# AUGRU keys of a recommendation model: transposed two steps ahead in six buffers, and gathered a step earlier

## The chip, the cores and the metric

The kernel runs on one NeuronCore of a Trainium2 chip. The metric is the time of one execution on the device in microseconds; a smaller number is better. The engines are named as in the profile: PE is TensorE (its weight loads are a row of their own, PEld), DVE is VectorE, ACT is ScalarE, POOL is GpSimd, SP is SyncE. All arithmetic is in 32-bit floats.

## The reference

1024 samples each have a history of 100 items with 128 features. Three stages follow one another: a GRU over the history, attention over its outputs, and a second recurrent network (AUGRU) over the same outputs, whose update gate is scaled by the attention. The state that AUGRU has at the end of each sample's sequence goes into a small network that gives the score.

```python
# gru: h_t for all t, from zero
keys = gru_seq                                   # [1024, 100, 128]
feat = concat([keys, q, keys - q, q * keys])     # q: item_embedding
score = mlp(feat, [512 -> 80, 80 -> 40, 40 -> 1], relu)
attn = softmax(where(mask == 1, score, -inf), over t)
pooled = einsum('bt,btd->bd', attn, keys)
att_seq = pooled.T[:100]

def augru_step(h, x_t, a_t):                     # x_t = keys[:, t], a_t = att_seq[t]
    r = sigmoid(concat([h, x_t]) @ Wr.T + br)
    u = sigmoid(concat([h, x_t]) @ Wu.T + bu)
    h_hat = tanh(concat([h * r, x_t]) @ Wh.T + bh)
    u = a_t[:, None] * u
    return (1 - u) * h + u * h_hat

attention_feature = aug_out[b, sequential_length[b] - 1]
comb = concat([user, item, hist_sum, item * hist_sum, attention_feature])
return mlp(comb, [640 -> 200, 200 -> 80, 80 -> 1], sigmoid)
```

The weight `a_t` of an AUGRU step is a feature of the pooled vector, so AUGRU can't start before all keys are pooled.

## The kernel before

The 128 features lie on the partitions, the samples along the free dimension. The 1024 samples are two halves (`NH = 2`) of `HB = 512` columns, which are worked on in turn so that the engines have one half to work on while the other waits. `gru_phase` runs the first recurrence and the attention over both halves and stores the keys in DRAM, by groups of steps: `READ` is the number of steps in each group (4, 4, then eleven times 8, then 4) and `FIRST` the first step of each (0, 4, 8, 16, ... 88, 96). `augru_phase`, which the change touches, runs the second recurrence. It begins at about 1440 us of the profiled 2085.5.

For AUGRU the samples are sorted by length, longest first, so that a late step computes only the columns of samples that are still alive. `widths[t]` is the number of columns that step `t` computes in each half: it falls from 512 to 96. (A value computed on the device picks one of three such plans; with these inputs it is the first, the narrowest.)

How a key reaches PE. The sort makes it necessary to gather the rows of the keys from DRAM, each row holding one sample's keys, or a 32-feature part of them, for all steps of a group. `load_rows` (L144) does this with indirect DMAs that POOL issues (L159), each after a small copy on POOL from the tile `rest` of the step then running (L158), which paces them. `gathers(q)` is the sequence of all such DMAs of group `q`, and `spread(q)` says how many of them are issued after each half step, so that the group is complete some steps before its first use. The rows are then transposed, one step and half at a time, by `load_key` (L996 to L1013) into a tile `k3` of 128 x 512 from the pool `qp3`. For the first two groups (`q < WHOLE`, steps 0 to 7) PE transposes blocks of 128 x 128 into the single PSUM buffer of the pool `pa3` (L1006) and ACT copies the result (L1007). For all later steps DVE does it alone, in blocks of 32 x 32 (L1010).

The step itself is `half_step(t, i)` for half `i`. The engines run in program order: the program is written out by hand, no scheduler reorders it. Each half step does the following.

- PE closes `ph` of the other half, the half step before (`ph<-r`, L1024), then `pr` and `pu` of its own half (`pr<-h`, `pu<-h`, L1024); ACT takes the tanh `c` of the first and the sigmoids of the others.
- DVE multiplies `u` and `c` of the other half (L1048), makes `r` (L1050), updates the other half's state `h3` (L1052), scales `pu` with the attention (L1058) and makes `rest` (L1061).
- PE opens the three gates of the half step after (`open_gates`, `pr<-k`, `ph<-k`, `pu<-k`, L1020): the part of the matmul that depends only on the key.
- The attention weights of two steps later are loaded (`load_att`), and the key of one step later in the same half is transposed (`load_key(t + 1, i)`).

So PE has six matmuls in each half step, each with its own weights; the profile shows each as a pair (`x2`).

Ahead of the loop stand, in this order: the keys of step 0, ACT's four stores of the last `pooled` rows, the gathers of the attention weights in sorted order (`att_r`, L135), the first step (L947), the keys of step 1, the gates of step 1, its first weights, and the gathers of group 1. Scores of samples that have ended are computed beside the loop in small portions (`predict`, L1080 to L1148); they gather and scatter through POOL too (L1088).

The tile pools of the AUGRU phase take over the memory that the pools of the GRU phase used; where an AUGRU tile lies over a GRU tile, its first writer waits until that tile's last reader is done.

Of the kernel before, what the change touches and what calls it, by code (L numbers as in the profile page):

```python
# [21 lines left out]
T = 100  # L22
HB = 512
NH = B // HB
# [31 lines left out]
FIRST = [sum(READ[:q]) for q in range(len(READ))]  # L56
# [16 lines left out]
def kernel(ctx: ExitStack, tc: tile.TileContext, a: dict, out: bass.AP):  # L73
# [70 lines left out]
    def load_rows(q, i, width, tiles):  # L144

        n = READ[q]
        if q < WHOLE:
            tag = "whole" if q else "once"
            r = rows[q, i] = tiles.tile([P, GH, n * P], F32, tag=tag, name="rows", bufs=NH)
            for g in range(GH):  # L150
                gather(r[:, g, :], keys_d[q], g, i)
                yield
            return
        r = rows[q, i] = tiles.tile([P, KH, n * R], F32, tag="rows", name="rows")
        for k in range(-(-width // R)):
            if later.get("pace") is not None:

                nc.gpsimd.tensor_copy(r[:, k, 0:1], later["pace"])  # L158
            nc.gpsimd.indirect_dma_start(  # L159
                out=r[:, k, :],  # L160
                out_offset=None,
                in_=keys_d[q],
                in_offset=bass.IndirectOffsetOnAxis(ap=idx_k[:, k, i : i + 1], axis=0),
            )
            yield

    def all_of(steps):
        for _ in steps:
            pass
# [755 lines left out]
    def augru_phase(pools, widths, alive):  # L925


        wp = pools.enter_context(tc.tile_pool(name="wp3", bufs=3))
        qp = pools.enter_context(tc.tile_pool(name="qp3", bufs=4))
        sp = pools.enter_context(tc.tile_pool(name="sp3", bufs=2))  # L930
        kp = pools.enter_context(tc.tile_pool(name="kp3", bufs=4))
        ps = pools.enter_context(tc.tile_pool(name="ps3", bufs=7, space=PSUM))
# [37 lines left out]
        def first_state(i, p):  # L970
            weight_row(0, i, p)
            u, h = gates[i]
            nc.vector.tensor_mul(p, p, u)
            nc.vector.tensor_mul(h3[i], p, h)

        def first_weights(i, p):
            weight_row(1, i, p)
            at = att[1, i] = wp.tile([P, HB], F32, name="at", bufs=6)
            nc.scalar.copy(at, p)

        def store_weights(i, p):

            for g in range(GH):
                nc.tensor.transpose(p[:, ts(g, P)], sorted_rows[i][:, g, :], ident)
            rows_t = wp.tile([P, HB], F32, name="att_t", bufs=2)
            nc.vector.tensor_copy(rows_t, p)
            nc.sync.dma_start(out=att_d[i], in_=rows_t[:T, :])
            load_att(2, i)

        def load_att(t, i):  # L990
            w = widths[t]
            at = wp.tile([P, HB], F32, name="at", bufs=6)
            nc.sync.dma_start(
                out=at[:, :w], in_=att_d[i][t, :w].partition_broadcast(P)
            )
            att[t, i] = at  # L996

        def load_key(t, i):

            q = max(j for j, first in enumerate(FIRST) if first <= t)  # L1000
            w, n, r = widths[t], t - FIRST[q], rows[q, i]
            k = qp.tile([P, HB], F32, name="k3")
            if q < WHOLE:
                p = pa.tile([P, HB], F32, tag="a", name="pk3")
                for g in range(-(-w // P)):
                    nc.tensor.transpose(p[:, ts(g, P)], r[:, g, ts(n, P)], ident)  # L1006
                nc.scalar.copy(k[:, :w], p[:, :w])  # L1007
            else:
                w = -(-w // R)
                nc.vector.transpose(  # L1010
                    k.rearrange("p (k r) -> p k r", r=R)[:, :w, :], r[:, :w, ts(n, R)]
                )
            keys[t, i] = k  # L1013

        def open_gates(t, i):

            k = keys.pop((t, i))[:, : widths[t]]
            for m, name in ((wr, "pr"), (wh, "ph"), (wu, "pu")):
                p = opened[t, i, name] = bank(name)[:, : widths[t]]
                nc.tensor.matmul(p, lhsT=m[:, 1, :], rhs=k, start=True, stop=False)  # L1020

        def close_gate(t, i, name, m, v):
            p = opened.pop((t, i, name))
            nc.tensor.matmul(p, lhsT=m[:, 0, :], rhs=v, start=False, stop=True)  # L1024
            return p

        def open_state(t, i):

            r, u, rest = resets.pop((t, i))
            ph = close_gate(t, i, "ph", wh, r)  # L1030
            c = wp.tile([P, HB], F32, name="c3")[:, : widths[t]]
            nc.scalar.activation(c, ph, AF.Tanh, bias=later["bh"])  # L1032
            states[i] = u, c, rest, h3[i][:, : widths[t]]

        def half_step(t, i):


            w, h = widths[t], h3[i][:, : widths[t]]
            before, after = ((t - 1, 1), (t, 1)) if i == 0 else ((t, 0), (t + 1, 0))
            if before in resets:  # L1040
                open_state(*before)
            pr = close_gate(t, i, "pr", wr, h)
            pu = close_gate(t, i, "pu", wu, h)
            nc.scalar.activation(pr, pr, AF.Sigmoid, bias=later["br"])
            nc.scalar.activation(pu, pu, AF.Sigmoid, bias=later["bu"])
            state = states.pop(1 - i, None)
            if state is not None:
                nc.vector.tensor_mul(state[0], state[0], state[1])  # L1048
            r = wp.tile([P, HB], F32, name="r3")[:, :w]
            nc.vector.tensor_mul(r, h, pr)  # L1050
            if state is not None:
                nc.vector.tensor_sub(state[3], state[0], state[2])  # L1052
            if t == 1 and i == 0:
                store_weights(0, pa.tile([P, HB], F32, tag="a", name="pw"))
                first_state(1, spare)
            elif t == 1:
                first_weights(1, spare)
            nc.vector.tensor_mul(pu, pu, att.pop((t, i))[:, :w])  # L1058
            rest = wp.tile([P, HB], F32, name="rest")[:, :w]

            nc.vector.scalar_tensor_tensor(  # L1061
                out=rest, in0=pu, scalar=1.0, in1=h, op0=ALU.subtract, op1=ALU.mult
            )
            later["pace"] = rest[:, 0:1]
            resets[t, i] = r, pu, rest
            if after[0] < T and (*after, "pr") not in opened:
                open_gates(*after)
            if t == 1 and i:
                store_weights(1, spare)
            if t + 2 < T:  # L1070
                load_att(t + 2, i)
            if t + 1 < T:
                load_key(t + 1, i)

        def last_state(i):
            u, c, rest, h = states.pop(i)
# [73 lines left out]
        def gathers(q):  # L1150
            for i in range(NH):
                yield from load_rows(q, i, widths[FIRST[q]], kp)

        def spread(q):


            ahead = 2 if widths[FIRST[q]] > HB // 2 else 3
            n = NH * -(-widths[FIRST[q]] // R)
            slots = NH * (FIRST[q] - (FIRST[q - 1] if q > 2 else 1) - ahead)
            done = [-(-j * n // slots) for j in range(slots + 1)]  # L1160
            return [b - a for a, b in zip(done, done[1:])]

# [12 lines left out]
        first_state(0, pa.tile([P, HB], F32, tag="a", name="first"))  # L1175
        first_weights(0, spare)
        all_of(gathers(1))
        ahead, due = gathers(2), spread(2)
        jobs, final = [], None
        for t in range(1, T):  # L1180
            if t in FIRST[2:-1]:
                all_of(ahead)
                ahead, due = gathers(FIRST.index(t) + 1), spread(FIRST.index(t) + 1)
            for i in range(NH):
                half_step(t, i)
                for _ in range(due.pop(0) if due else 0):
                    next(ahead, None)

                for n, job in enumerate(list(jobs)):
                    job[0] += 1  # L1190
                    if n == 0 and job[0] > 2 * G and next(job[1], job) is job:
                        jobs.remove(job)
            left = alive[t + 1] if t + 1 < T else 0
            for g in range(1, HB // PR):
                if left <= g * PR < alive[t]:
                    jobs.append([0, predict(g)])
                    if left:
                        next(jobs[-1][1])
            if t == T - G:
                final = predict(0, last=True)  # L1200
                next(final)
# [10 lines left out]
    def augru(n):  # L1212
        with ExitStack() as pools, tc.manual_schedule():
            augru_phase(pools, WIDTHS[n], ALIVE[n])
# [75 lines left out]
```

## Time and profile before

| | |
|---|---|
| time, median of 3 runs | 2083.58 us (2083.48 to 2083.83) |
| span of the profiled execution | 2085.5 us |
| instructions | 26811 |
| mean granted clock of TensorE | 0.993 |
| DMA traffic | 205.09 MB, mean 98 GB/s |
| read from and written to HBM | 147.16 MB, 54.40 MB |

The five engines' busy shares stand in the profile line with which the prediction begins. A busy share is an average over stages: in the GRU phase and in the first two thirds of the AUGRU phase PE has no room at all, in the last third of the AUGRU phase, where the steps are narrow, it has a little. A row of a timeline gives the start in microseconds, the duration, the engine, the line of the kernel, the operation, the tile written and those read, the shapes, and in brackets the idle time of the engine before it and what ended that.

### The profile page before, as it was taken

The page shows a single profiled execution, that of the slowest core. Times are in us where ns is not written, and L with a number is a line of the kernel's source. Part 1 is how long each engine was busy: PE and PEld are TensorE (multiplying, and loading weights), DVE is VectorE, ACT ScalarE, POOL GpSimd, SP SyncE. Part 2 cuts the span into 40 slices and gives each one's busy share as a digit, 9 for nine tenths or more (in the row PEclk, how much of TensorE's full clock was granted, in tenths as well). Part 3 has the DMA queues.
Part 4 walks back from the last instruction along what each step waited for, and adds up shares of the span by engine and source line. Part 5 has one row for each costly group of instructions (what it writes and reads, how often), then busy time and mean ns, then how long its engine had stood idle before and what let it go on. Part 6 is the DMA issues. An engine that isn't in the chain of part 4 may idle for free. (4 is left out here: it accounts for less than half of the span.)

```text
span 2085.5 us, 26811 instructions
## 1 busy us (share of the span) xinstructions
PE 2039.8 (98%) x8320; PEld 980.6 (47%) x8320; DVE 1755.5 (84%) x3050; ACT 831.7 (40%) x1516; POOL 1304.6 (63%) x1306
## 2 busy tenths in 40 slices
PE   8999999999999999999999999997899999999997
PEld 3343333333333333333333333333444556678897
DVE  6888999989989888989889899997467777888786
ACT  3334343333434333433333343333343444445454
POOL 0234939579796959595969687986635444444332
PEclk9999999999999999999999999998999999999999
DMA  4633233332234334333433222332533333334331
GB/s 119 114 93 100 90 102 110 95 98 84 89 106 112 109 103 121 110 95 110 132 98 102 82 81 89 102 93 72 150 95 110 97 93 96 98 98 97 78 73 35
DMA packets 254324, 205.09 MB, mean 98 GB/s; under 512 B 75814, under 2 KB 216842, under 8 KB 254170
## 3 DMA queue, kind: packets, MB, share of 16 engines
q1 hardware_dynamic: 239738, 170.57, 29.2%
q0 software_dynamic: 12320, 32.44, 5.6%
q8 instruction: 68, 1.11, 0.2%
q14 instruction: 86, 0.70, 0.1%
q10 hardware_dynamic: 2112, 0.26, 0.1%
HBM read 147.16 MB, written 54.40 MB: 97 GB/s over the span
## 5 line engine op out<-in xcount | busy, mean ns | idle before, releaser
L490 PE MATMUL ps<-x,wih 128*128 128x512 f32 x1200 | 592.6, 603 | 4.0 <-DMA x<-in_hist_x 4.0
L490 PE MATMUL ps<-hn,whh 128*128 128x512 f32 x1188 | 574.4, 592 | 0.0
L490 PEld LDWEIGHTS ps<-x,wih 128*128 128x128 f32 x1200 | 220.9, 191 | 327.5 <-issue 253.0
L490 PEld LDWEIGHTS ps<-hn,whh 128*128 128x128 f32 x1188 | 225.7, 190 | 284.1 <-issue 275.8
L476 POOL TENSOR_TENSOR xm<-x,m 128x512 f32<-128x512 f32 x200 | 247.2, 1236 | 136.3 <-DMA m<-mask_d 136.0
L521 ACT ACTIVATE ps<-ps,bih 128x512 f32<-128x512 f32 x200 | 132.4, 662 | 486.6 <-DVE ps L520 486.6
L502 ACT ACTIVATE r<-ps,brz 128x512 f32<-128x512 f32 x200 | 137.5, 687 | 372.9 <-PE ps L490 372.1
L477 POOL TENSOR_TENSOR hist<-hist,xm 128x512 f32<-128x512 f32 x200 | 266.7, 1333 | 15.7
L587 POOL TENSOR_TENSOR pooled<-pooled,kw 128x512 f32<-128x512 f32 x191 | 254.4, 1332 | 15.0
L586 POOL TENSOR_TENSOR kw<-kt,e 128x512 f32<-128x512 f32 x191 | 219.3, 1148 | 70.3 <-DVE e L759 70.2
L159 POOL DMA_INDIRECT rows<-keys_d,idx_k x208 | 202.3, 973 | 83.8 <-POOL rows L158 53.0
L563 DVE TENSOR_TENSOR kq<-hn,item 128x512 f32<-128x512 f32 x200 | 228.5, 1182 | 0.0
L650 PE MATMUL pm<-hn,wk 128*32 128x512 f32 x1200 | 212.0, 596 | 3.5 <-ACT q L233 1.8
L650 PE MATMUL pm<-kq,wkq 128*32 128x512 f32 x1200 | 209.6, 592 | 0.0
L1032 ACT ACTIVATE c<-ph,bh 128x96 f32<-128x96 f32 (+42 forms) x198 | 96.9, 489 | 262.2 <-PE ph L1024 227.7
L650 PE MATMUL pm<-mv,w 128*32 128x512 f32 (+1 forms) x808 | 196.5, 598 | 1.4 <-DVE e L740 1.4
L158 POOL COPY rows<-rest 128x1 f32<-128x1 f32 x208 | 39.1, 188 | 222.1 <-DVE rest L1061 218.1
L1048 DVE TENSOR_TENSOR pu<-pu,c 128x96 f32<-128x96 f32 (+42 forms) x197 | 88.8, 451 | 103.6 <-ACT c L1032 85.0
L684 DVE TENSOR_TENSOR f<-pm,q 128x512 f32<-128x512 f32 x200 | 128.3, 683 | 51.2 <-PE pm L650 51.1
L525 DVE TENSOR_TENSOR d<-hn,ps 128x512 f32<-128x512 f32 x198 | 135.9, 687 | 34.8 <-ACT ps L521 32.5
L526 DVE TENSOR_TENSOR d<-ps,d 128x512 f32<-128x512 f32 x200 | 138.4, 692 | 23.6 <-ACT ps L522 6.4
L520 DVE TENSOR_TENSOR ps<-ps,u 128x512 f32<-128x512 f32 x200 | 140.0, 700 | 21.6 <-PE ps L490 0.5
(180 smaller groups left out, 3028.3 us busy)
## 6 DMA issues: line engine op xcount, KB each, us to landing
x<-in_hist_x SPq DMA_DIRECT2D x212, 256.0 KB
keys_d<-kt SPq DMA_DIRECT2D x46, 1024.0 KB
m<-mask_d SPq DMA_DIRECT2D x200, 128.0 KB
keys_d<-kt SPq DMA_DIRECT2D x64, 64.0 KB
rows<-keys_d,idx_k POOLq DMA_INDIRECT x208
s_b<-mv SPq DMA_DIRECT2D x200, 8.0 KB
mask_i<-in_mask SPq DMA_DIRECT2D x8, 200.0 KB
at<-att_d SPq DMA_DIRECT2D x32, 48.0 KB
```

The source lines that it names most:

```text
L159: nc.gpsimd.indirect_dma_start(out=r[:, k, :], out_offset=None, in_=keys_d[q], in_offset=bass.IndirectOffsetOnAxis(ap=idx_k[:, k, i : i + ...
L476: nc.gpsimd.tensor_mul(d, x, m)
L477: nc.gpsimd.tensor_add(acc, acc, d)
L490: nc.tensor.matmul(p, lhsT=w[:, g, :], rhs=v, start=(j == 0), stop=(j == len(parts) - 1),)
L502: nc.scalar.activation(r, pr, AF.Sigmoid, bias=brz[:, 0:1])
L520: nc.vector.tensor_add(pi, pi, u)
L525: nc.vector.tensor_sub(d, h, pi)
L526: nc.vector.tensor_mul(d, pz, d)
L563: nc.vector.tensor_mul(kq, h, item[:, self.cols])
L586: eng.tensor_mul(d, k, w)
L587: eng.tensor_add(acc, acc, d)
L650: nc.tensor.matmul(p[i][s, :], lhsT=w[:, s], rhs=v, start=start, stop=stop)
```

## The change

The key of a half step is transposed two steps ahead, where it was one, and the pool of the key tiles grows from four buffers to six, since two more tiles are alive at any time. The keys of step 2 are therefore transposed ahead of the loop. Since a group's rows are needed one step earlier, the loop turns to the next group one step earlier too (`t + 1` in place of `t`), and `spread` counts with that. It is for the wait of PE for a key: with the change a gate's key has been ready a whole step when PE opens the gate.

```diff
-        qp = pools.enter_context(tc.tile_pool(name="qp3", bufs=4))
+        qp = pools.enter_context(tc.tile_pool(name="qp3", bufs=3 * NH))
...
-            if t + 1 < T:
-                load_key(t + 1, i)
+            if t + 2 < T:
+                load_key(t + 2, i)
...
         def spread(q):
-            ahead = 2 if widths[FIRST[q]] > HB // 2 else 3
+            ahead = 3 if widths[FIRST[q]] > HB // 2 else 4
             n = NH * -(-widths[FIRST[q]] // R)
-            slots = NH * (FIRST[q] - (FIRST[q - 1] if q > 2 else 1) - ahead)
+            slots = NH * (FIRST[q] - (FIRST[q - 1] - 1 if q > 2 else 1) - ahead)
...
         all_of(gathers(1))
+        for i in range(NH):
+            load_key(2, i)
         ahead, due = gathers(2), spread(2)
         jobs, final = [], None
         for t in range(1, T):
-            if t in FIRST[2:-1]:
+            if t + 1 in FIRST[2:-1]:
                 all_of(ahead)
-                ahead, due = gathers(FIRST.index(t) + 1), spread(FIRST.index(t) + 1)
+                ahead, due = gathers(FIRST.index(t + 1) + 1), spread(FIRST.index(t + 1) + 1)
             for i in range(NH):
                 half_step(t, i)
```

## The prediction

> **What bounds the kernel now.** I read the page first, then the busy times by stretch, then the waits of the last stretch, then the timelines of PE and DVE inside it, and last the timeline of the hand-over between the two phases.
>
> ```profile
> PE 2039.8 (98%) x8320; PEld 980.6 (47%) x8320; DVE 1755.5 (84%) x3050; ACT 831.7 (40%) x1516; POOL 1304.6 (63%) x1306
> ```
> PE carries the kernel as a whole. The change touches only the AUGRU phase, which starts near 1440 us, so nothing before that moves. Its stretches (us; busy time and instructions of PE, PEld, DVE, ACT, POOL; clock; DMA):
>
> ```profile
> 1480.00:1880.00 400.00, 400.00 (x1300) 236.68 (x1299) 306.88 (x585) 178.71 (x321) 187.09 (x319) 1.00 0.37 103
> 1880.00:2072.00 192.00, 185.31 (x1235) 170.78 (x1234) 155.48 (x581) 99.10 (x307) 68.93 (x112) 1.00 0.32 74
> 1968.00:2012.00 44.00, 43.13 (x317) 39.87 (x317) 37.51 (x150) 23.33 (x79) 14.34 (x23) 1.00 0.31 74
> ```
> From 1480 to 1880 PE never rests. In the timeline a half step there takes just its six matmul pairs: 3.97 us at 394 columns, with 0.03 us over. No wait can be saved there. From 1880 on the steps are narrow, PE rests 6.7 us by its records, and DVE is busy 81 to 85%. Who PE waits for there (us in total, times, longest; PEld is its weight load, which sees the wait first):
>
> ```profile
> POOL rows L158 <- DVE rest L1061: 68.4, 18, 16.1
> ...
> PEld pr L1020 <- DVE k L1010: 6.7, 18, 1.0
> ```
> So the key transposition, which stands last on DVE in each half step, is the wait that ends last. The timelines show it in one step at 144 to 148 columns:
>
> ```profile
> 1989.04 0.41 PE L1024 MATMUL pu<-h,wu 128*128 128x144 f32 x2
> 1989.56 0.51 PE L1020 MATMUL pr<-k,wr 128*128 128x144 f32 x2
> 1989.91 0.41 PE L1020 MATMUL ph<-k,wh 128*128 128x144 f32 x2
> ```
> ```profile
> 1987.83 0.32 DVE L1048 TENSOR_TENSOR pu<-pu,c 128x148 f32<-128x148 f32 x1 [0.19 <-issue]
> ...
> 1989.17 0.34 DVE L1010 STREAM_TRANSPOSE k<-rows 128x160 f32<-128x160 f32 x1
> 1989.43 0.31 DVE L1048 TENSOR_TENSOR pu<-pu,c 128x148 f32<-128x148 f32 x1
> ...
> 1991.26 0.32 DVE L1048 TENSOR_TENSOR pu<-pu,c 128x144 f32<-128x144 f32 x1 [0.18 <-issue]
> ```
> Pairs of matmuls start 0.24 us apart, but pr<-k starts 0.52 after pu<-h, at 1989.56, when the transposition of 1989.17 has ended (1989.51). DVE itself goes from 1987.83 to 1989.43 without a pause, then rests 0.18 us.
>
> The hand-over, by engine:
>
> ```profile
> 1439.76 0.59 ACT L1007 COPY k<-pk 128x512 f32<-128x512 f32 x1 [0.38 <-ACT part L625]
> 1441.55 0.59 ACT L1007 COPY k<-pk 128x512 f32<-128x512 f32 x1 [1.21 <-PE pk L1006]
> ```
> ```profile
> 1446.52 1.27 POOL L587 TENSOR_TENSOR pooled<-pooled,kw 128x512 f32<-128x512 f32 x1
> 1454.59 0.99 POOL L135 DMA_INDIRECT att_r<-pooled_d,idx  x1 [6.81 <-PE ph L947]
> ```
> ```profile
> DVE first L973 <- PE first L962: 13.4, 1, 13.4
> ...
> PE pk L1006 <- DVE att_t L986: 6.7, 1, 6.7
> ```
> ACT copies the keys of step 0 while POOL still pools. Later PE stands for 6.7 us before the keys of step 2.
>
> **What the Trainium skill says.** "Perfetto Trace Analysis", Identifying the Most-Contended Engine, says that matmul busy time is no measure of how full PE is, and its summary of profiler windows that the end of a matmul is estimated. The trace agrees: the PE row is 100% busy in 1480 to 1880 and 98% in 1968 to 2012, where starts show waits. I therefore count starts, not busy time. The same page, Optimization Strategy, says that the same gap repeating on the engine that should be full can mean too few buffers; here the gap repeats, but its releaser is an instruction that comes late. "TensorE: Matmul & The Clock Gate", LDWEIGHTS, gives a load of 128 columns as 128/1.2 = 107 ns; the timeline at 96 columns has pairs 0.22 us apart, 110 ns each, so below about 130 columns a half step stays near 6 x 0.22 = 1.33 us. Its section What's actually happening says that PE runs at half clock after about 3.4 us of idling; the granted clock from 1440 to 1456 is 0.58.
>
> **The change part by part.**
>
> 1. The keys are transposed two steps ahead (L1072). DVE runs the same L1010 at the same place, only for a later step: 184 before, 184 after. Nothing is added to DVE. PE's pr<-k then reads a tile two half steps older, so the wait on L1010 goes. To size it I took all starts of PE from 1880 on and subtracted what each matmul takes where nothing is waited for. The excess at pr<-k (its first matmul and, as its weight load is late too, its second) is 1.5 us in 1880:1946, 0.5 in 1946:1958, 1.6 in 1958:1968, 5.1 in 1968:2012, 1.8 in 2012:2030, 3.2 in 2030:2072: 13.7 us in all, of about 24 us that PE loses there.
> Not all of it comes back. At 144 to 148 columns DVE's six operations need 1.60 us (1987.83 to 1989.43) and 1.83 - 0.18 = 1.65: 3.25 us a step, against 3.43 now and 12 x 0.245 = 2.94 for PE. DVE takes over as the bound, and 0.18 us a step is the gain. For the 12 steps of 1968:2012 that is 2.2 us; I take 2.4, as the wider ones gain more. At 96 columns a step takes 1.39 + 1.49 us or more, and DVE needs about 1.28 a half step, so PE's own 1.39 can be reached: I take 1.9 of the 3.2. Of 1.8, where the two meet, 0.9; of 0.5, 0.3. The 3.1 us in the disturbed stretches follow late gates, ACT waiting up to 2.5 us for PE: I take 0.9. Sum 6.4 us; bounds 3 (half) and 11 (nearly all).
>
> 2. Six buffers instead of four. The pool qp3 grows from 8 to 12 KiB a partition and now reaches over the end of the old pool hp into the old pool wp, which holds POOL's kw tiles. In the built program the first copy k<-pk on ACT then waits for the last pooled add on POOL, which it did not. POOL ends at 1446.52 + 1.27 = 1447.8 instead of the copy starting at 1439.76. Behind it are queued the second copy and ACT's four stores of pooled_d; PE's transposition between the copies and its first gates wait for ACT. From first copy to end of the second is 1442.14 - 1439.76 = 2.38 us, so the stores start at about 1450.2 instead of 1449.3, and the gathers of att_r on POOL about 1 us later. PE's first gates start about 1.5 us later than 1448.0. I take 1.5 us for the hand-over (0.9 to 3.5, if the half clock lasts one more 3.4 us spell).
>
> 3. Two key transpositions before the loop: PE 4 matmuls, ACT a copy, PE 4, ACT a copy, through the single buffer of pa3, ahead of the first pr<-h. Each is 0.6 us on PE and 0.59 on ACT, 2.4 us in a chain. PE's 6.7 us of idling just after hide part of it; the trace doesn't show what ends them (DVE waits 4.2 us more on something named remote), so 0 to 2.4 us; I take 1.0. In return the half steps of t = 6 lose their 4 matmuls, 0.43 us each, where PE was full: -0.9 us.
>
> 4. Gathers a step earlier (lines 1157 to 1185). The same count, 208, spread over as many half steps for all groups but the first, which goes from 10 slots of 3 to 4 to 8 slots of 4. Four gathers with their pacing copies take 4 x 1.44 = 5.8 us against a half step of 5.5, so POOL runs even with PE for 46 us and ends near 1528; the first use is near 1535. Rows of the group before are free two steps ahead, as before. Zero, hidden beside PE's matmuls.
>
> Sum: -6.4 + 1.5 + 1.0 - 0.9 = -4.8 us, 2083.6 - 4.8 = 2078.8 us.
>
> **Rivals.**
>
> A. The wait is removed in full and the hand-over hides in the 6.7 us of idling: -11 + 0.5 = 2073 us. For it: PE would reach 2.94 us a step. Against: DVE's 3.25 us a step.
>
> B. The wait comes back under another name: PE, freed at pr<-k, stands at ph<-r for L1050 on DVE instead. Gain 3 us, hand-over at 3: 2083.5 us, no change. For it: DVE is 85% busy and ph<-r already waits in places. Against: in the step shown r ended at 1989.96 and ph<-r started at 1990.40, 0.4 us to spare.
>
> C. Slower: the hand-over costs 6 us, since two more trips between PE and ACT fall where PE's results are slow to be seen, and the shifted gathers meet the predictions' gathers on POOL so that the disturbed stretches grow by 3 us while 3 are gained: 2089.5 us. For it: the unexplained 4.2 us wait. Against: the idling is there before, too.
>
> **How the numbers follow.** Forecast 0.42, A 0.2, B 0.28, C 0.1. The forecast's spread of about 4 us around 2078.8 lies some three fifths under 2079.4 (0.2% faster), A wholly, B hardly: faster 0.52, same 0.38, slower 0.10. The range takes A and B in and leaves out about a tenth on each side: 2073 to 2086.
>
> **What would show it.** Right: no PE wait on k L1010 from 1880 on; step time at 144 columns near 3.25; DVE without idling there; the first k copy near 1447.9; the second half's first pr<-h about 2.5 us after 1478.88. Wrong: a wait of ph<-r on L1050 of equal size, a DVE wait on gathered rows near t = 6, or the AUGRU loop starting over 5 us later.

## The result, and the profile after

| | before | after |
|---|---|---|
| time, median of 6 runs | 2083.78 us (2083.48 to 2084.77) | 2077.12 us (2076.60 to 2078.01) |
| span of the profiled execution | 2085.5 us | 2075.2 us |

The ratio is 0.9968, with a 95% interval of 0.9955 to 0.9980: 6.7 us faster. The two profiled spans differ by more, 10.3 us, because the profiled execution of before was longer than most: with its 2087.38 us it lies 3.6 us above its own median, that of after (2077.06 us) at its median.

The page of the changed kernel, busy time by engine, and its busy times by stretch (us; PE, PEld, DVE, ACT, POOL, clock, DMA):

```profile
PE 2030.8 (98%) x8320; PEld 980.9 (47%) x8320; DVE 1753.8 (85%) x3050; ACT 832.2 (40%) x1516; POOL 1307.9 (63%) x1306
```
```profile
1480.00:1880.00 400.00, 400.00 (x1289) 235.67 (x1288) 307.31 (x585) 177.78 (x319) 190.86 (x324) 1.00 0.36 104
1880.00:2072.00 192.00, 182.58 (x1264) 174.70 (x1262) 157.43 (x589) 102.47 (x315) 66.92 (x109) 0.98 0.32 74
1968.00:2012.00 44.00, 42.73 (x336) 40.85 (x335) 38.24 (x157) 25.01 (x85) 16.61 (x28) 1.00 0.31 73
```
The instructions are the same in number; 336 matmuls instead of 317 fit into 1968 to 2012, in part because the narrower steps have come up sooner. From 1480 to 1880 PE is full, as before. Its waits from 1880 on (us in total, times, longest):

```profile
POOL rows L158 <- DVE rest L1061: 70.8, 18, 14.4
...
PEld ph L1024 <- DVE r L1050: 3.9, 8, 0.8
...
PE ph L1024 <- DVE r L1050: 2.0, 4, 0.5
```
The wait of pr<-k for the transposition (6.7 us at PEld before) is no longer in the list. The one that stays is ph<-r for `r`. The same place in the timeline, at 144 columns:

```profile
1985.07 0.41 PE L1024 MATMUL pr<-h,wr 128*128 128x144 f32 x2
1985.21 0.31 DVE L1061 SCALAR_TENSOR_TENSOR rest<-pu,h 128x144 f32<-128x144 f32 x1
1985.44 0.34 DVE L1010 STREAM_TRANSPOSE k<-rows 128x160 f32<-128x160 f32 x1
1985.55 0.35 ACT L1044 ACTIVATE pr<-pr,br 128x144 f32<-128x144 f32 x1
1985.56 0.40 PE L1020 MATMUL pr<-k,wr 128*128 128x138 f32 x2
1985.70 0.30 DVE L1048 TENSOR_TENSOR pu<-pu,c 128x144 f32<-128x144 f32 x1
1985.93 0.30 DVE L1050 TENSOR_TENSOR r<-h,pr 128x144 f32<-128x144 f32 x1
1986.29 0.51 PE L1024 MATMUL ph<-r,wh 128*128 128x144 f32 x2
1986.64 0.40 PE L1024 MATMUL pr<-h,wr 128*128 128x138 f32 x2
```
pr<-k now starts 0.24 us after pu<-h (1985.32) and beside the transposition, which is for a later step. A half step, from one pr<-h to the next, takes 1985.07 to 1986.64, 1.57 us, in both halves. Before, the halves took 1.85 and 1.57 at this width, so a step went from 3.42 to 3.14 us. DVE shows no idle time (no row of it has a bracket), and a second chain is as long: pr<-h to its sigmoid 0.48, to r 0.38, to ph<-r 0.36, to the pr<-h of the other half 0.35, together 1.57. The experiments take the two apart.

The hand-over:

```profile
1447.71 0.59 ACT L1007 COPY k<-pk 128x512 f32<-128x512 f32 x1 [8.43 <-POOL pooled L587]
1447.90 1.29 DVE L919 TENSOR_TENSOR s_b<-used,pooled 128x512 f32<-128x512 uint8 x2
...
1449.56 2.06 ACTq L1167 DMA_DIRECT2D pooled_d<-s_b  x4
...
1454.67 0.99 POOL L135 DMA_INDIRECT att_r<-pooled_d,idx  x1 [6.99 <-PE pk L1006]
...
1464.33 0.63 PE L1006 MATMUL pk<-ident,rows 128*128 128x128 f32 x4 [0.78 <-DVE h L974]
1464.78 0.96 POOL L135 DMA_INDIRECT rows<-keys_d,idx  x1 [0.30 <-issue]
1465.96 0.59 ACT L979 COPY at<-spare 128x512 f32<-128x512 f32 x1 [8.73 <-DMA att_r<-pooled_d,idx]
...
1468.11 0.59 ACT L1007 COPY k<-pk 128x512 f32<-128x512 f32 x1 [1.57 <-remote]
1468.75 1.11 PE L1006 MATMUL pk<-ident,rows 128*128 128x128 f32 x4 [3.80 <-ACT k L1007]
```
The first key copy does wait for POOL, to 1447.71, but POOL's gathers of the attention weights then start 6.99 us after its last addition, where it was 6.81. Further down the new transposition of PE is over by 1464.96, and ACT's copy of it starts at 1468.11, 3.2 us later. I call this a late answer: an instruction starts microseconds after what it waits for has ended, and its own engine is free.

Late answers matter for reading all the numbers below. The experiments were run in four sets, each with the kernel before beside them. It took 2083.91 us beside e1 to e4, 2090.19 beside e5 to e8, 2066.79 beside e9 to e11 and 2066.61 beside e12, so a time is compared only with the kernel before of its own set. In the profiles of e1 to e8, which all ran on one chip, there are late answers (in e7 only as long as rows are gathered); in those of e9 to e11, on a second chip, and of e12, on a third, hardly any.

### The profile page after: what moved, and what is told of

The parts are those of the page before. It is cut to its first block, busy times and chain, and to the rows that moved or that the text cites. A ratio compares the mean times of both kernels' runs of the same rounds, so it can differ in the third digit from the quotient of the medians.

```text
span 2075.2 us, 26811 instructions
## 1 busy us (share of the span) xinstructions
PE 2030.8 (98%) x8320; PEld 980.9 (47%) x8320; DVE 1753.8 (85%) x3050; ACT 832.2 (40%) x1516; POOL 1307.9 (63%) x1306
```

## The experiments

Half-step times are differences between the starts of pr<-h on PE in a timeline. "Loop from 262 columns" is the time from the 101st such start to the last but one.

**e1: the pool alone.**

```diff
 # on the kernel before
-        qp = pools.enter_context(tc.tile_pool(name="qp3", bufs=4))
+        qp = pools.enter_context(tc.tile_pool(name="qp3", bufs=3 * NH))
```


> The kernel before with six key buffers and nothing else. If the wait of ACT's first key copy for POOL's last pooled add delays the start of the AUGRU loop, as the prediction has it, the time is 1.5 us above before (about 2085.3). If the wait is hidden behind the store of the pooled rows and the gathers of the attention weights, as the trace of the changed kernel suggests (its first att_r gather starts at 1454.67 where it was 1454.59), it is within 0.3 us of before. In both cases the first k copy starts near 1447.7.

Measured: 2084.53 us, ratio 1.0004 (0.9995 to 1.0012). The interval takes in both expectations, so the time does not decide between them. The loop from 262 columns takes 186.11 us here, with the order of instructions of before, whose own profile has 191.08. These 5 us lie in half steps that are late in the one profile and prompt, or less late, in the other.

**e2: the extra buffers where nothing waits for POOL.**

```diff
 # on the changed kernel
-        qp = pools.enter_context(tc.tile_pool(name="qp3", bufs=3 * NH))
+        qp = pools.enter_context(tc.tile_pool(name="qp3", bufs=2 * NH))
...
+        qx = pools.enter_context(tc.tile_pool(name="qx3", bufs=NH))   # after kp3
...
-            k = qp.tile([P, HB], F32, name="k3")
+            k = (qx if t % 3 == 2 else qp).tile([P, HB], F32, name="k3")
```


> The changed kernel with the two extra key buffers in a pool of their own behind the row tiles, used by every third step, so that the first pool stays at 8 KiB and the first k copy does not wait for POOL. If the wait cost what the prediction says, 1.5 us come back: about 2075.6. If it is hidden, 2077 as the changed kernel.

Measured: 2076.77 us, ratio 0.9965 (0.9953 to 0.9977). The interval is 5 us wide and does not decide about 1.5 us. The profile does: it shows the wait gone and what that brings.

```profile
1439.07 0.58 ACT L1008 COPY k<-pk 128x512 f32<-128x512 f32 x1 [0.39 <-ACT part L625]
```
```profile
1453.83 0.99 POOL L135 DMA_INDIRECT att_r<-pooled_d,idx  x1 [6.75 <-issue]
```
POOL waits 6.75 us before the gathers instead of 6.99. The wait costs 0.24 us here, not 1.5: the gathers need the stored rows, and DVE makes those rows (`s_b`, L919) from 1447.90 to 1449.19 in any case.

**e3: no transposition ahead of the loop.**

```diff
 # on the changed kernel
-            if t + 2 < T:
+            if t + 1 < FIRST[WHOLE]:
+                load_key(t + 1, i)
+            if FIRST[WHOLE] <= t + 2 < T:
                 load_key(t + 2, i)
...
-        for i in range(NH):
-            load_key(2, i)
```


> The changed kernel, but the keys that PE transposes (steps 1 to 7) are made one step ahead as before, only those that DVE transposes two steps ahead; nothing stands ahead of the loop for step 2. If the two transpositions ahead of the loop cost what the traces show (the third half step starts at 1488.00 for 1485.90, less 0.87 us won back at step 6), 1.2 to 1.3 us come back: about 2075.8. If the start is set by something else (the slow answers while POOL gathers), no change: 2077.

Measured: 2077.05 us, ratio 0.9968 (0.9956 to 0.9981). Nothing comes back that can be told from the noise, which is wider than the 1.2 us in question. The first pr<-h starts at 1464.93 instead of 1469.66, yet the third at 1487.32, for 1488.00 in the changed kernel. The two half steps before it took 22.4 us instead of 18.3, so something else sets when they end.

**e4: the gathers alone, and e5: the keys alone.**

```diff
 # e4: on the kernel before; e5: the same lines taken back from the changed kernel
-            ahead = 2 if widths[FIRST[q]] > HB // 2 else 3
+            ahead = 3 if widths[FIRST[q]] > HB // 2 else 4
...
-            slots = NH * (FIRST[q] - (FIRST[q - 1] if q > 2 else 1) - ahead)
+            slots = NH * (FIRST[q] - (FIRST[q - 1] - 1 if q > 2 else 1) - ahead)
...
-            if t in FIRST[2:-1]:
+            if t + 1 in FIRST[2:-1]:
```


> The kernel before with the gathers a step earlier and nothing else: keys one step ahead, four buffers. If all the gain is the wait for the key, 2083.8 as before, and the waits of pr<-k on L1010 stay at about 6.7 us. If the shifted gathers are what made the disturbed stretches (PE's results seen late around 1890, 1930 and 1960 us) smaller, 2 to 4 us less than before: 2080 to 2082.

> The changed kernel with the gathers at the steps they had before (complete three steps, or two in the wide part, before their first use; still in time for a transposition two steps ahead). If the key alone makes the gain, 2077 as the changed kernel. If the shifted gathers have a part in it, 1 to 2 us more: 2078 to 2079. If the rows now come late, DVE waits on them at the first step of a group and PE behind it: over 2080.

Measured: e4 2082.77 us, ratio 0.9994 (0.9986 to 1.0003); e5 2083.36 us beside a before of 2090.19, ratio 0.9962 (0.9948 to 0.9975). The waits of e4 from 1880 on still have the transposition:

```profile
PEld pr L1020 <- DVE k L1010: 4.6, 16, 0.6
```
In e5 it is not there. So the keys carry the gain and the gathers none that can be measured (the interval of e4 leaves room for at most 3 us): the original placing was in time for keys two steps ahead.

**e6: DVE relieved.**

```diff
 # on the changed kernel: no transposition from step 68 on
+            if t > 67:
+                keys[t, i] = kept[i]
+                return
-            k = qp.tile([P, HB], F32, name="k3")
+            k = kept[i] = qp.tile([P, HB], F32, name="k3")
```


> The changed kernel without the key transpositions of steps 68 to 99 (those steps use the keys of step 67, so the output differs): DVE has five operations in a half step instead of six, PE the same six matmul pairs. If DVE is the bound of the narrow steps now, as predicted, the half steps at 170 to 112 columns lose the 0.1 to 0.18 us that they stand over PE's own time, about 2.5 us in all, and the time is 2074 to 2075. If the round of PE, ACT and DVE through one half sets the step, whatever DVE's load, they stay as they are: 2077.

Measured: 2081.70 us beside 2090.19, ratio 0.9948 (0.9935 to 0.9962). By the time alone this is what the first theory expects, but the interval overlaps that of e5, and the timeline says otherwise:

```profile
1992.14 0.41 PE L1028 MATMUL pr<-h,wr 128*128 128x144 f32 x2
...
1992.62 0.35 ACT L1048 ACTIVATE pr<-pr,br 128x144 f32<-128x144 f32 x1
...
1992.76 0.32 DVE L1052 TENSOR_TENSOR pu<-pu,c 128x144 f32<-128x144 f32 x1 [0.16 <-issue]
...
1993.00 0.30 DVE L1054 TENSOR_TENSOR r<-h,pr 128x144 f32<-128x144 f32 x1
...
1993.36 0.51 PE L1028 MATMUL ph<-r,wh 128*128 128x144 f32 x2
...
1993.71 0.40 PE L1028 MATMUL pr<-h,wr 128*128 128x138 f32 x2
```
DVE now rests, and the half step still takes 1.57 us, with the same four intervals. So the round pr<-h, sigmoid, r, ph<-r is a bound without the transposition's load on DVE.

**e11: the round shortened, DVE's load kept.** (Run in a later set.)

```diff
 # on the changed kernel: no sigmoid of the reset gate from step 68 on
-            nc.scalar.activation(pr, pr, AF.Sigmoid, bias=later["br"])
+            if t < 68:
+                nc.scalar.activation(pr, pr, AF.Sigmoid, bias=later["br"])
```


> The changed kernel without the sigmoid of the reset gate from step 68 on (r is the state times the gate's sum, so the output differs). DVE keeps its six operations in a half step and PE its six matmul pairs; what is shorter by some 0.4 us is the round pr<-h, sigmoid on ACT, r on DVE, ph<-r, pr<-h of the other half. If that round is the bound of the narrow steps (0.48 + 0.38 + 0.36 + 0.35 = 1.57 us in the trace, and the same 1.57 in e6 with DVE relieved), the half step at 144 columns falls from 1.57 to about 1.45, and the time by some 2.5 us to 2074 or 2075. If DVE is the bound, it stays at 1.57 and the time at 2077.

Measured: 2059.24 us beside 2066.79, ratio 0.9960 (0.9947 to 0.9974). Neither expectation holds at 144 columns: the half step takes 1.54 us, where e9 of the same set has 1.57.

```profile
1971.33 0.41 PE L1024 MATMUL pr<-h,wr 128*128 128x144 f32 x2
...
1971.70 0.33 DVE L1010 STREAM_TRANSPOSE k<-rows 128x160 f32<-128x160 f32 x1
...
1971.96 0.30 DVE L1049 TENSOR_TENSOR pu<-pu,c 128x144 f32<-128x144 f32 x1
...
1972.17 0.29 DVE L1051 TENSOR_TENSOR r<-h,pr 128x144 f32<-128x144 f32 x1
...
1972.53 0.51 PE L1024 MATMUL ph<-r,wh 128*128 128x144 f32 x2
...
1972.87 0.40 PE L1024 MATMUL pr<-h,wr 128*128 128x138 f32 x2
```
`r` no longer waits for ACT but for its turn on DVE, which has no idle time. So there are two bounds 0.03 us apart at this width, 1.57 of the round and 1.54 of DVE, and each alone hides what the removal of the other would bring. At 96 columns the half step goes from 1.38 or 1.39 to 1.35, near the 1.33 that six pairs of PE 0.22 us apart would take. Removing both at once was not tried.

**e7: no gathers from group 9 on.**

```diff
 # on the changed kernel, in load_rows
+        if q > 8:
+            rows[q, i] = rows[8, i]
+            return
```


> The changed kernel without the row gathers from group 9 on (steps 64 to 99 use the rows of group 8, so the output differs): POOL has only the predictions' gathers and scatters from about 1910 us on. If runs of gathers on POOL are what makes PE's results late, the half steps with 0.7 to 1.5 us over PE's time (five of them in the changed kernel from 1950 us on, 4.9 us together) are gone: 2072 to 2073. If they come from the predictions or from the loads of the attention weights, they stay: 2077.

Measured: 2076.27 us beside 2090.19, ratio 0.9927 (0.9913 to 0.9940), 7.1 us less than e5 of the same set. No half step from 1880 on takes over 0.15 us more than its usual time. In the changed kernel such a half step looks like this (ph<-r of a usual one and of a late one, and the ACT instruction that waits for each):

```profile
1950.33 0.48 PE L1024 MATMUL ph<-r,wh 128*128 128x190 f32 x2
...
1950.86 0.42 ACT L1032 ACTIVATE c<-ph,bh 128x190 f32<-128x190 f32 x1 [0.81 <-PE ph L1024]
...
1952.40 0.58 PE L1024 MATMUL ph<-r,wh 128*128 128x184 f32 x2
...
1953.10 0.19 POOL L158 COPY rows<-rest 128x1 f32<-128x1 f32 x1
...
1953.56 0.97 POOL L159 DMA_INDIRECT rows<-keys_d,idx_k  x1 [0.27 <-issue]
...
1953.83 0.42 ACT L1032 ACTIVATE c<-ph,bh 128x184 f32<-128x184 f32 x1 [1.56 <-PE pu L1024]
```
It is 0.53 us from matmul to tanh in the one and 1.43 in the other. POOL issues one gather after the other there, with no more than a pacing copy and some 0.3 us between them.

**e8: group 1 gathered after the first half step.**

```diff
 # on the changed kernel
-        all_of(gathers(1))
...
                 half_step(t, i)
+                if t == 1 and i == 0:
+                    all_of(gathers(1))       # its first gather behind a copy from rest
```


> The changed kernel with the eight gathers of group 1 issued after the first half step, behind a copy from its tile rest, instead of straight behind the gathers of the attention weights. If POOL's gathers make PE's results late, the first two half steps, which took 18.3 us from 1469.66 to 1488.00, lose their late answers: the third half step starts at about 1483 instead of 1488, and the time is about 2072. If the start is bound by its own chain of PE, ACT and DVE, nothing is won: 2077, or up to 2 us more as the gathers of group 2 now stand behind.

Measured: 2087.03 us beside 2090.19, ratio 0.9986 (0.9979 to 0.9992), slower than the changed kernel (0.9968), and than e5 of the same set (0.9962). The first half was right: pr<-h at 1467.36 has its sigmoid at 1468.42, and the third half step starts at 1479.11 instead of 1488.00. But then the rows are missing:

```profile
1490.51 0.33 PE L1008 MATMUL pk<-ident,rows 128*128 128x128 f32 x1 [0.63 <-DMA rows<-keys_d,idx]
...
1497.23 0.58 ACT L1009 COPY k<-pk 128x502 f32<-128x502 f32 x1 [6.38 <-remote]
...
1498.43 0.70 DVE L1050 TENSOR_TENSOR pu<-pu,c 128x512 f32<-128x512 f32 x1 [6.06 <-ACT c L1034]
```
The fourth to the seventh half step take 13.8 us more than in the changed kernel, part of it waiting for the rows, part of it late answers, as the gathers of groups 1 and 2 now run one behind the other beside them.

**e9, e10 and e12: ways around the late answers.**

```diff
 # e9: on the changed kernel
+            ahead = 3
+            slots = NH * (FIRST[q] - (FIRST[q - 1] - 2 if q > 2 else 1) - ahead)
...
+            if t + 2 in FIRST[2:-1]:
 # e10: on e3
+        group = gathers(1)
+        for _ in range(GH):
+            next(group)
         sorted_rows = [gather_weights(i) for i in range(NH)]
...
+                if t == 1 and i == 0:
+                    all_of(group)
```


> The changed kernel with the same gathers spread over 14 half steps of a group instead of 10 (the loop turns to the next group two steps ahead, the group is complete three steps ahead), so about one in a half step where it was one to two. If it is runs of gathers one behind the other that make PE's results late, the half steps with 0.7 to 1.5 us over PE's time are fewer or gone: 2072 to 2074. If each gather costs by itself, or the number of them counts, no change: 2077; if the rows come too late, DVE waits on them and the time is above 2079.

> The kernel e3_no_preload with the first half's four gathers of group 1 ahead of those of the attention weights, where POOL stood idle from 1447.8 to 1454.6, and the second half's four behind the first half step, paced by its rest. If gathers on POOL made the answers of the first two half steps late and the rows were too late in e8 only for their number, the third half step starts near 1479 as in e8, where it was 1487 to 1488, and nothing waits for rows after it: 2068 to 2070. If the rows still come late, half steps 4 to 6 wait as in e8 and the gain is spent: 2077 or more.

> The edits of e2, e3, e9 and e10 together on the changed kernel: extra buffers in a pool of their own, PE's keys one step ahead, gathers of group 1 in POOL's idle time, the other gathers spread evenly. Where PE's results come late while POOL gathers (as in the first traces), the third half step starts near 1478 instead of 1488 and the half steps with 0.7 us and more over PE's time shrink: 10 to 13 us under the changed kernel, a ratio to before of 0.990 to 0.992. Where they do not come late (as in the traces of e9 to e11), there is nothing to win at these places and the ratio is that of the changed kernel, 0.996 to 0.998.

Measured: e9 2060.86 us, ratio 0.9972 (0.9961 to 0.9982), and e10 2060.46 us, 0.9968 (0.9956 to 0.9980), beside 2066.79; e12 2060.21 us, 0.9968 (0.9955 to 0.9980), beside 2066.61. All three have the ratio of the changed kernel. They can't tell what they were made for, because in these sets there were no late answers to avoid. e11 has the start of the changed kernel, with the same gathers behind the attention weights, and its answers are prompt:

```profile
1464.60 0.63 PE L1006 MATMUL pk<-ident,rows 128*128 128x128 f32 x4 [0.79 <-DVE h L974]
1465.03 0.96 POOL L135 DMA_INDIRECT rows<-keys_d,idx  x1 [0.30 <-issue]
1465.26 0.59 ACT L1007 COPY k<-pk 128x512 f32<-128x512 f32 x1 [0.83 <-PE pk L1006]
```
0.66 us from matmul to copy, where the changed kernel's own profile has 3.78. The third half step starts at 1478.14 in e11, 1477.45 in e9, 1477.86 in e10, 1476.85 in e12. No version was shown to beat the changed kernel.

## Why the prediction was right

It said 2078.8 us and named the reason, the key wait; 2077.12 was measured.

**Step 1, the key wait: right in mechanism; 6.4 us forecast, about 6.4 measured.** For each half step I took the shortest time among three profiles with keys one step ahead (before, e1, e4) and among four with keys two ahead (after, e2, e3, e5), all from runs with late answers, and summed the differences:

| columns | forecast, us | measured, us |
|---|---|---|
| 262 to 200, and 180 to 174 (the disturbed stretches) | 0.9 | 0.25 + 0.61 = 0.86 |
| 194 to 184 | 0.3 | 0.44 |
| 170 to 112 | 2.4 | 2.39 |
| 108 to 96, first ten half steps | 0.9 | 1.22 |
| 96, the rest | 1.9 | 1.48 |

Most late answers fall out in this way. Three half steps at 96 columns are late in all seven profiles and make 0.4 us of the sum, so 6.0 to 6.4 us is what it shows. With the profiles of e9 and e12 it would be 7.8, but there these three half steps are prompt, and no profile with keys one step ahead comes from such a set: most of the difference would be late answers counted as gain.

That the sum is met so closely is in part luck, since its rows are off by up to 0.4 us either way. At 96 columns one half took 1.48 to 1.56 us and the other 1.39, and with the wait gone nearly all take 1.39. The bound at 144 columns was named as DVE with 3.25 us a step. Measured are 3.14, so DVE's operations can stand closer together than they did before. And DVE is one of two bounds: e6 shows that the round through the reset gate holds the same 1.57 us with less load on DVE. Rival B's mechanism, ph<-r waiting for L1050, is there, but it is not the whole gain: six pairs of PE, 0.235 us apart, would take 1.41 us, so it keeps 0.16 us of a half step.

**Step 2, the pool: the wait was found, its cost mis-sized.** 1.5 us were forecast. The first copy moved to 1447.71 as worked out (1447.8). The forecast then had the stores of the pooled rows start after the end of ACT's second copy, at 1450.2. They start at 1449.56, 0.06 us after its start. Before, they started at 1449.31, when DVE had just made the rows:

```profile
1447.99 1.29 DVE L919 TENSOR_TENSOR s_b<-used,pooled 128x512 f32<-128x512 uint8 x2
...
1449.31 2.05 ACTq L1167 DMA_DIRECT2D pooled_d<-s_b  x4
```

From the end of these rows to the first gather of the attention weights it is 5.24 to 5.31 us in the profiles without the wait (before, e2, e4) and 5.45 to 5.48 in those with it (e10 and e12 gather in another order and are left out). So the wait costs about 0.2 us. The second copy of ACT and the first gates of PE, 1.25 us later than before, lie beside POOL's own wait of 7 us.

**Step 3, the transpositions ahead of the loop.** The gain at step 6 is as forecast: the two half steps went from 5.39 and 5.37 to 4.95 and 4.93 us, -0.88 for -0.9. The cost, 1.0 forecast, can't be settled to better than a microsecond. In the profiles with late answers the start of the loop moves by up to 3 us between kernels with no reason in their edits (third half step at 1485.90 in before, 1487.09 in e1, 1488.81 in e4, 1486.58 in e5), and e3's time is that of the changed kernel. For the same reason one sign that the prediction named says little: the second half's first pr<-h came at 1480.29, 1.4 us after 1478.88 and not 2.5, and e4 has it at 1480.03 with the old keys.

**Step 4, the gathers: nothing, as forecast** (e4 and e5).

So -6.4 from the keys, 0.2 from the pool and -0.9 at step 6 make -7.1, and the timed -6.7 leaves 0.4 for the transpositions ahead of the loop. That is a remainder and not a measurement: the interval of the ratio is 5 us wide. The fifteenth half step starts at 1551.73, for 1550.51 in the profile of before but 1551.69 in that of e1. The forecast fell 1.9 us short of the measured gain, 1.3 of it at the pool and, by this remainder, 0.6 at the transpositions.

**What the prediction read wrongly** is the disturbed stretches of before. It took them as part of the schedule. They are late answers, which differ between two profiles of one schedule (191.08 and 186.11 us), and are not a property of the kernel alone.

## What to carry to other kernels

A wait at the end of an engine's order is removed by doing that work a step earlier, at the price of buffers, and what it gives is read from the spacing of starts, not from busy time. Add up the time of the next chain before naming the next bound, and look for a second one of the same length: each hides the other. And compare two profiles of one schedule before explaining a stretch of one.

## What was not expected of the hardware

Results of PE could reach ACT late while POOL issued indirect DMAs one behind the other: 3.78 us from the start of a transposition to its copy, where another set of runs had 0.66 with the same gathers at the same times. Taking gathers away removes it (e7, and the first two half steps of e8), so in those sets it came with the gathers, but they don't suffice. Whether it is their issue on POOL or their transfers was not separated. Beside it the kernel before ranged from 2066.6 to 2090.2 us between sets of runs. What differs between the sets stays open. The two with late answers ran on one chip and the two without on two others, so the chip itself may be the cause; but the two sets of the first chip also differ from each other, by 6 us for the kernel before. Whether a different order of gathers would avoid late answers stays open too.

e6 ended 0.14% below e5 of its set though its half steps show no gain; the intervals overlap, and whether less work on DVE has to do with the late answers was not tried.
